# Letting GpSimd gather up to 24 tiles ahead of the sums in the middle of a graph layer, and closing up to eight at the end

## The chip, the cores and the metric

The kernel runs on one core of a Trainium2 chip. The metric is the device time of one execution in microseconds. Before the change three runs gave 1995.14, 1996.98 and 1998.15 us, so the median is 1996.98 us.

## What is computed

A layer of a relational graph network over 12500 nodes with 256 features, 212500 edges sorted by target, and 8 edge types, in float32:

```python
h   = maximum(layernorm(x), 0)
hx  = einsum('ni,rio->rno', h, weight)            # 8 types
agg = segment_sum(hx[edge_type, src], dst)        # 212500 edges
out = x + agg * 0.5**0.5 + h_bias + (h @ loop_weight) * 0.5**0.5
```

## The kernel before, in words

**Tiles and units.** The edges are cut into 1583 tiles of up to 128 edges; two tiles make a unit. The main loop runs once over the tiles, `t` from 0 to 1582. In step `t` the 128 source rows of a tile (1 KB each) lie in an SBUF tile `msg`, a one-hot matrix `oh` over (target, type) lies beside it, and TensorE multiplies them (`edge_sums`, L972) into a PSUM bank `ps`. VectorE adds the bank of a unit to a ring of accumulators `acc` (`add_sums`, L998). When a group of 128 nodes is complete, TensorE multiplies its accumulators by the 8 weight matrices and the loop weight into `po` (L1154), VectorE adds `x` (L1167, L1168), and SyncE writes every four groups out (L1173). Those products are dealt out between the sums of later tiles. All engine orders are written out by hand; no scheduler changes them.

**How the rows come.** For most tiles GpSimd issues one indirect DMA (`gather`, L885), 128 rows from `h32`, the normed table in HBM (the first 100 gathers read `x` and norm it on the core). For every 28th tile, 45 in all, GpSimd is passed by: `begin_fetch` and `load_sources` issue the 128 rows one by one, 64 from SyncE's queue and 64 from ScalarE's (L908). They are put into those queues 36 tiles ahead of their use, from eight steps later on at four per queue and step.

**What sets the lead.** At the top of step `t` the loop issues gathers until `goal(t)` is reached, and each of them is made to wait for the last unit whose sums have been written into the program (`latest["unit"]`):

```python
while gathered < min(NT, goal(t)):
    gather(gathered)
```

So a gather for tile `t + lead` does not start on the chip before the sums of about tile `t - 1` are done: `lead` is how far GpSimd may run ahead. It is 64 (`AHEAD`) up to tile 170 (`NARROW`), then shrinks by one tile in five (`SLOPE`) to `NEXT`.

**Two other waits of the same instructions.** The gathers signal their landing on eight semaphores in turn. In the built program each gather also waits until the gather eight places before it has landed, whatever `lead` is. And the message buffers are 33 pairs, handed out in turn (`room`), so the first row of a tile that is fetched row by row waits for the sums of the tiles that last used its pair. The three waits stand like this in the listing of the program before (GpSimd's gathers of tiles 612 and 613, ScalarE's first row of tile 587; semaphore values written out as tiles):

```
POOL gather of tile 612        waits: gather eight before landed; sums through tile 603
POOL gather of tile 613        waits: gather eight before landed
ACT  first row of tile 587     waits: sums through tile 503
```

Of the kernel before, what the change touches and what calls it, by code (L numbers as in the profile page):

```python
# [55 lines left out]
STEEP = 2  # L56
NARROW = 170
SLOPE = 5
NEXT = 8

SINGLE = 28
FETCH = 4
# [177 lines left out]
def kernel(  # L240
# [20 lines left out]
    NT = plan.NT  # L261
# [42 lines left out]
    with ExitStack() as main:  # L304
# [587 lines left out]
        def goal(t):  # L892

            lead = max(NEXT, AHEAD - max(0, t - NARROW) // SLOPE)
            return min(t + lead + 1, STARTED + STEEP * (t // PAIR * PAIR))

        def load_sources(t, r0, engine):
# [302 lines left out]
        with tc.manual_schedule():  # L1200
# [115 lines left out]
            for t in range(NT):  # L1316
# [3 lines left out]
                while gathered < min(NT, goal(t)):  # L1320
                    gather(gathered)
                    gathered += 1
# [122 lines left out]
```

## Time and profile before

| | us |
|---|---|
| median of three runs | 1996.98 |
| the profiled execution's own time | 1995.13 |
| its span in the profile | 1993.4 |
| TensorE matmul busy (share of the span) | 1779.7 (89%) |
| TensorE weight load busy | 1557.2 (78%) |
| GpSimd busy | 1461.3 (73%) |
| VectorE busy | 1378.2 (69%) |
| ScalarE busy | 136.1 (7%) |

A row of a group view names line, engine, operation, output and inputs and count, then busy time, mean duration in ns of one, and the idle time of the engine just before these instructions with what ended most of it. In a timeline row the figures ahead are start and duration in us, and the bracket holds the idle time just before the instruction and what ended it; "issue" means that nothing in the profile ended it. "POOL" is GpSimd, "SPq" and "ACTq" are the DMA-issuing sequencers of SyncE and ScalarE.

### The profile page before, as it was taken

Reading aid. Unit: us, or ns where it says so; the run is one execution under the profiler, and the core shown is the slowest. Engines: PE = TensorE matmul, PEld = TensorE weight load, DVE = VectorE, ACT = ScalarE, POOL = GpSimd, SP = SyncE. Lnnn points to the kernel's source line nnn. Section 1 sums busy time; section 2 is a strip of 40 time slices with the busy share of each in tenths; the row PEclk is TensorE's granted clock in tenths of the full one; section 3 lists DMA queues with packets and bytes.
Section 4 is the critical chain, followed back from the end, with each engine's and each line's share of the span. In section 5 each row is a group of like instructions: output and inputs, shape, how many; then the busy total and the mean of one; then the engine's idle time right before and its main releaser. Section 6 shows DMA issues by size and latency. Waiting matters only on the chain. (4 is left out here: it accounts for less than half of the span.)

```text
span 1993.4 us, 39889 instructions
## 1 busy us (share of the span) xinstructions
PE 1779.7 (89%) x10171; PEld 1557.2 (78%) x10171; DVE 1378.2 (69%) x3288; ACT 136.1 (7%) x243; POOL 1461.3 (73%) x1563
## 2 busy tenths in 40 slices
PE   2458999999999988999999999999999999899998
PEld 2347899899978876888878887878877887787986
DVE  6779767779856777656569666668766667765752
ACT  6764200000000000000000000000000000000000
POOL 7677777777767777777777777777777777777774
PEclk9559999999999999999999999999999999999999
DMA  8993434444444544444444444444444344444432
GB/s 269 354 289 98 143 106 138 141 136 120 139 119 118 150 130 114 136 130 123 140 119 142 131 119 139 131 129 139 132 121 142 109 141 131 117 142 118 130 106 77
DMA packets 157314, 279.57 MB, mean 140 GB/s; under 512 B 34799, under 2 KB 107864, under 8 KB 157080
## 3 DMA queue, kind: packets, MB, share of 16 engines
q0 software_dynamic: 73824, 201.69, 34.7%
q1 hardware_dynamic: 75896, 72.34, 11.7%
q10 hardware_dynamic: 7360, 2.97, 0.8%
q8 instruction: 80, 1.31, 0.3%
q14 instruction: 154, 1.26, 0.2%
HBM read 251.26 MB, written 25.60 MB: 139 GB/s over the span
## 5 line engine op out<-in xcount | busy, mean ns | idle before, releaser
L885 POOL DMA_INDIRECT msg<-h,gidx x1438 | 1364.7, 949 | 470.0 <-issue 353.8
L972 PEld LDWEIGHTS ps<-oh,msg 128*128 128x128 f32 x6332 | 995.2, 197 | 344.8 <-DMA msg<-h,gidx 206.5
L972 PE MATMUL ps<-oh,msg 128*128 128x176 f32 (+1 forms) x6332 | 1107.2, 305 | 176.2 <-DMA msg<-h,gidx 99.4
L1154 PE MATMUL po<-w,acc 128*128 128x256 f32 x3136 | 883.1, 386 | 9.4 <-DVE acc L998 9.4
L998 DVE TENSOR_TENSOR acc<-acc,ps 128x352 f32 x792 | 409.9, 518 | 369.9 <-PE ps L972 357.8
L1154 PEld LDWEIGHTS po<-w,acc 128*128 128x128 f32 x3136 | 532.1, 192 | 42.8 <-DVE acc L998 11.4
L935 DVE TENSOR_TENSOR oh<-fixed,cols 128x704 f32<-128x704 f32 x397 | 349.2, 880 | 0.0
L1036 DVE SCALAR_TENSOR_TENSOR acc<-types,pt 128x256 f32<-128x256 bf16 (+1 forms) x688 | 247.5, 413 | 85.0 <-PE pt L1018 79.8
L885 POOL DMA_INDIRECT msg<-in_x_dram,gidx x100 | 94.8, 948 | 38.8 <-issue 30.3
L1154 PE MATMUL po<-wl,self_t 128*128 128x256 f32 x392 | 111.7, 409 | 3.4 <-DVE acc L998 1.7
L1154 PEld LDWEIGHTS po<-wl,self_t 128*128 128x128 f32 x392 | 72.0, 205 | 12.9 <-DVE acc L998 2.5
L823 ACT ACTIVATE msg<-msg,shift,rstd 128x256 f32<-128x256 f32 x100 | 50.7, 586 | 4.2 <-DVE shift L820 3.4
L823 ACT ACTIVATE xt<-xt,shift,rstd 128x256 f32<-128x256 f32 x98 | 50.0, 587 | 7.0 <-DVE shift L820 5.6
L1167 DVE TENSOR_TENSOR xr<-xr,po 128x256 f32<-128x256 f32 x98 | 40.5, 414 | 13.3 <-PE po L1154 12.5
L793 DVE BATCH_NORM_STATS2 stats<-xt 128x6 f32<-128x256 f32 x98 | 34.3, 412 | 19.1 <-DMA xt<-in_x_dram 18.3
L1090 DVE CAST types<-pt 128x512 bf16<-128x512 f32 x22 | 15.2, 692 | 44.8 <-PE pt L1086 44.8
L1023 DVE COPY self_t<-pt 128x256 f32<-128x256 f32 x98 | 40.8, 416 | 6.8 <-PE pt L1018 5.5
L1018 PE MATMUL pt<-ident,hr 128*128 128x128 f32 x196 | 38.1, 277 | 7.5 <-DMA hr<-h 6.4
L1168 DVE TENSOR_TENSOR xr<-xr,po 128x256 f32<-128x256 f32 x98 | 41.2, 421 | 3.4
L429 DVE TENSOR_SCALAR moves<-fixed 128x271 int32<-128x271 int32 (+1 forms) x90 | 40.5, 451 | 3.1 <-DVE acc L998 2.1
L431 DVE COPY_PREDICATED fixed<-moves,fixed 128x311 int32<-128x311 int32 (+14 forms) x90 | 38.0, 422 | 3.1
L793 DVE BATCH_NORM_STATS2 stats<-msg 128x6 f32<-128x256 f32 x100 | 34.2, 410 | 0.0
(154 smaller groups left out, 321.1 us busy)
## 6 DMA issues: line engine op xcount, KB each, us to landing
msg<-h SPq DMA_DIRECT2D x2880, 1.0 KB
msg<-h ACTq DMA_DIRECT2D x2880, 1.0 KB
msg<-h,gidx POOLq DMA_INDIRECT x1438
xt<-in_x_dram SPq DMA_DIRECT2D x24, 512.0 KB
h<-xt SPq DMA_DIRECT2D x24, 512.0 KB
xr<-in_x_dram SPq DMA_DIRECT2D x24, 512.0 KB
hr<-h SPq DMA_DIRECT2D x24, 512.0 KB
out_dram<-xr SPq DMA_DIRECT2D x24, 512.0 KB
```

What stands on the lines that cost most here:

```text
L429: nc.vector.tensor_single_scalar(m, packed[:, :n], 1 << (bit + k), op=ALU.bitwise_and)
L793: in_run("stats", nc.vector.bn_stats(stats[:n, k, :], row), row is rows_[-1])
L823: nc.scalar.activation(row, row, AF.Relu, bias=shift[:n, j : j + 1], scale=rstd[:n, j : j + 1])
L885: i = nc.gpsimd.indirect_dma_start(out=msg[t], out_offset=None, in_=table[:, :], in_offset=bass.IndirectOffsetOnAxis(ap=gidx[b][:, at : at ...
L935: j = nc.vector.tensor_tensor(o[:, k : k + v, :i, :], iota_f.unsqueeze(1).unsqueeze(1).to_broadcast([P, v, i, C]), of.unsqueeze(3).to_broa ...
L972: j = nc.tensor.matmul(ps[:, c, :width], m[:, c * P : (c + 1) * P], o[:, :width], start=(i == 0 and c == 0), stop=(end and c == KC - 1))
L998: i = nc.vector.tensor_tensor(a, a, ps, op=ALU.add)
L1023: nc.vector.tensor_copy(got["self", g][:, :, :n], pst[:, :, :n])
L1036: i = nc.vector.scalar_tensor_tensor(acc[:, :, r, s0 : s0 + n], of, float(r + 1), pst[:, :, :n], op0=ALU.is_equal, op1=ALU.mult)
L1154: i = nc.tensor.matmul(got["out", g][:n], lhs, rhs, start=(r == R and c == 0), stop=(r == R - 1 and c == KC - 1))
L1167: nc.vector.tensor_add(rows_[:n, k, :], rows_[:n, k, :], outs[g % 2][:n, 1, :])
L1168: nc.vector.tensor_add(rows_[:n, k, :], rows_[:n, k, :], got["out", g][:n])
```

## The change

`NEXT` becomes 24, and a second line lets the lead close up towards the end of the edges to the new constant `CLOSE`, which is 8: by one tile in five over the last 120 tiles, and it stays at eight for the last forty or so.

```diff
-NEXT = 8
+NEXT = 24
+CLOSE = 8
...
         def goal(t):

             lead = max(NEXT, AHEAD - max(0, t - NARROW) // SLOPE)
+            lead = min(lead, max(CLOSE, (NT - t) // SLOPE))
             return min(t + lead + 1, STARTED + STEEP * (t // PAIR * PAIR))
```

In the built program no engine gets an instruction more or less, and on every engine the order of the instructions is the same. What differs is which semaphore values GpSimd, SyncE and ScalarE wait for. The three waits from above, after:

```
POOL gather of tile 612        waits: gather eight before landed; sums through tile 587
POOL gather of tile 613        waits: gather eight before landed
ACT  first row of tile 587     waits: sums through tile 519
```

## The prediction

> **What bounds the kernel now.** I read the page first, then the group of the message tile, then the chain that ended last.
>
> ```profile
> span 1993.4 us, 39889 instructions
> ...
> PE 1779.7 (89%) x10171; PEld 1557.2 (78%) x10171; DVE 1378.2 (69%) x3288; ACT 136.1 (7%) x243; POOL 1461.3 (73%) x1563
> ```
>
> ```profile
> L885 POOL DMA_INDIRECT msg<-h,gidx x1438: 940/946/1253, 136.4 to 1969.8; - x180
> L885 POOL DMA_INDIRECT msg<-in_x_dram,gidx x100: 940/946/1112, 4.9 to 135.2; - x100
> ```
>
> ```profile
> 1967.34 2.72 DMA msg<-h,gidx
> 1970.06 0.04 issue
> 1970.10 0.86 PE ps L972 x4
> ...
> 1979.93 7.78 PE po L1154 x36
> ...
> 1988.19 0.42 DVE xr L1168
> ```
>
> By busy time TensorE looks like the limit (89%) and GpSimd idle a quarter of the time. The other two fences correct that. GpSimd issues 1538 gathers; an undisturbed pair, below, starts 1.25 us apart (0.95 of work, 0.30 between), so they need 1537 x 1.25 = 1921 us, and from the first start (4.9) to the last (1969.8) pass 1964.9. GpSimd stands still for only some 44 us. The end hangs on its last gathers: landing, four matmuls, products that take until the last addition at 1988.2. So a microsecond that GpSimd gains in the middle and does not lose again is a microsecond at the end.
>
> TensorE can follow. These windows give TensorE's busy time first, GpSimd's fifth:
>
> ```profile
> 507.00:566.00 59.00, 57.87 (x355) 52.92 (x354) 44.04 (x97) 0.00 (x0) 40.38 (x43) 1.00 0.46 130
> 731.00:794.00 63.00, 54.27 (x294) 43.93 (x293) 50.02 (x120) 0.00 (x0) 45.54 (x48) 0.97 0.46 128
> 804.00:867.00 63.00, 58.87 (x347) 50.83 (x346) 41.10 (x91) 0.00 (x0) 47.50 (x51) 1.00 0.46 135
> 1846.00:1906.00 60.00, 59.01 (x351) 54.03 (x351) 39.29 (x88) 0.00 (x0) 44.42 (x47) 1.00 0.43 126
> ```
>
> At 804 to 867 GpSimd runs at its full rate (51 gathers in 63 us) and TensorE idles for 4 us: some 6% of room. At 507 it is 98% busy, but there it is still using up the early lead, and what GpSimd gains there it keeps as lead until TensorE has room again.
>
> **What the wait on the sums costs.** The lead was already 17 or more up to tile 400, so the change acts from about 440 us. GpSimd's waits from there to 1975 us, with the 0.30 that stands before every gather inside:
>
> ```profile
> POOL msg L885 <- issue: 298.0, 965, 2.1
> POOL msg L885 <- DMA msg<-h,gidx: 43.8, 109, 2.0
> POOL msg L885 <- PE ps L972: 37.3, 100, 1.5
> POOL msg L885 <- PE pt L1018: 5.4, 12, 1.7
> POOL msg L885 <- PE po L1154: 3.3, 9, 0.9
> ```
>
> Taking off 0.304 each (1.25 less the median 0.946): landings end 43.8 - 33.1 = 10.7 us of excess, TensorE 46.0 - 36.8 = 9.2 us over the three rows, and 298.0 - 293.4 = 4.6 us have no releaser. That is all that can be had after 440 us: 24.5 us.
>
> The 9.2 us bound the wait that the change loosens from above. From below stand the cases in which nothing else was due:
>
> ```profile
> 550.45 0.94 POOL L885 DMA_INDIRECT msg<-h,gidx  x1 [1.86 <-DMA msg<-h,gidx]
> 551.70 0.94 POOL L885 DMA_INDIRECT msg<-h,gidx  x1 [0.30 <-issue]
> ...
> 619.87 0.94 POOL L885 DMA_INDIRECT msg<-h,gidx  x1 [0.59 <-PE ps L972]
> ...
> 623.08 0.94 POOL L885 DMA_INDIRECT msg<-h,gidx  x1 [1.02 <-PE ps L972]
> ...
> 1173.78 0.94 POOL L885 DMA_INDIRECT msg<-h,gidx  x1 [1.12 <-PE ps L972]
> ...
> 1236.91 0.94 POOL L885 DMA_INDIRECT msg<-h,gidx  x1 [0.73 <-PE ps L972]
> ...
> 1871.09 0.94 POOL L885 DMA_INDIRECT msg<-h,gidx  x1 [1.67 <-PE pt L1018]
> ```
>
> Less 0.30 each, these five are 0.29 + 0.72 + 0.82 + 0.43 + 1.37 = 3.6 us. The other TensorE-ended waits lie among waits for landings, and behind them the landing of the gather eight before is due next; I count little of them and take **4 us**. The last, at 1871, is followed by no other stop. The closing of the lead costs nothing there: near tile 1502 it still stands at about 19 where eight stopped the gather, and for the last forty tiles it is what it was.
>
> **The wait for the gather eight before.** This wait stays, so a lead of 24 never means 24 gathers in flight; eight at 1.25 us is 10 us. The extra 16 tiles are used only when rows have landed and TensorE is late. Gathers that land in over 9 us stop GpSimd whatever the lead is: the 10.7 us. What makes them slow? Two stretches of the message tile, first 731 to 804 us, then 804 to 870:
>
> ```profile
> L908 ACTq DMA_DIRECT2D msg<-h x182: 227/228/787, 730.8 to 803.8; - x182
> ...
> L908 SPq DMA_DIRECT2D msg<-h x158: 227/228/480, 731.2 to 793.0; - x158
> L885 POOL DMA_INDIRECT msg<-h,gidx x54: 940/946/1131, 730.8 to 803.0; - x54
> ...
>   POOL msg L885: 10.0, 15
> ```
>
> ```profile
> L908 ACTq DMA_DIRECT2D msg<-h x140: 227/228/605, 803.8 to 869.7; - x140
> ...
> L908 SPq DMA_DIRECT2D msg<-h x128: 227/228/308, 819.7 to 869.6; - x128
> L885 POOL DMA_INDIRECT msg<-h,gidx x53: 942/946/1162, 804.2 to 869.5; - x53
> ...
>   POOL msg L885: 1.2, 4
> ```
>
> In the first, both row queues issue almost without a pause for 62 us and GpSimd waits 10.0 us for landings (with the 0.30); in the second they pause, and it waits 1.2. By the Trainium skill's "DMA: Bandwidth & Descriptors", section "Queues, rings and completion order", a DMA engine takes turns between the queues that have work, packet by packet, so a third busy queue would thin out the gathers' share; the two stretches agree. By that rule alone the landings quicken wherever one row queue pauses.
>
> **What the change does to the row queues.** No instruction moves, but the first row of a row-by-row tile now waits for sums 16 tiles later (tile 587: through 519, not 503), because the gathers take their buffers earlier. Why ScalarE's queue ran so long without a pause at 731:
>
> ```profile
> 632.72 49.77 ACTq L392 DMA_DIRECT2D spans<-in_dst_dram  x8
> 682.58 187.36 ACTq L908 DMA_DIRECT2D msg<-h  x435
> ...
> 1635.73 22.99 SPq L908 DMA_DIRECT2D msg<-h  x64
> ```
>
> It stood for 50 us at the loads of a block's spans, and then caught up with tiles whose buffers had long been free. A tile is 64 rows, 23 us of queue time (last row), in 28 tiles x 1.25 = 35 us: 12 us of pause when a queue is not behind. A gate 16 x 1.25 = 20 us later makes ScalarE's queue reach its gate one to two tiles sooner, and pause, while SyncE's, held up mostly at the output writes, goes on as before. So stretches with both queues busy for some 60 us should become stretches of 20 to 35 us, which GpSimd got through in the trace without a stop.
>
> What that is worth lies between nothing and all of 10.7 + 4.6 = 15.3 us; below nothing if the pauses fall badly (a rival). I take the middle, **8 us**: the catching up after the block at 1632 us begins so far behind that a gate 20 us later leaves its first stretch.
>
> Behind the later row issue the cover is the time to use: tile 587 is gated at the sums of 519 and used 68 tiles, 85 us, later, against 23 us of issue. SyncE's output write, its node loads and the rest of its queue stand behind these rows; they are due some 28 tiles, 35 us, before the rows' use at the earliest, so 85 - 35 = 50 us for 23 us of issue. I count nothing.
>
> **Sum.** 4 + 8 = 12 us off the profiled execution's 1995.13: 1983.1. That execution is the fast end of the three runs; the median lies 1.85 above it, so I add that: **1985 us**. Own range, from the median: 3.6 + 3 = 6.6 off gives 1990; all 24.5 off gives 1972.5.
>
> **Rivals.**
> *Only the wait on the sums goes.* The windows show that VectorE is busier where GpSimd stops: 75% and 79% at 507 and 731, 65% at 804 and 1846. The Trainium skill's "GPSIMD Engine Reference", section "Specifications", says that GpSimd shares its SBUF interfaces with VectorE; the trace cannot part that from the row queues, which are busy at the same times. If VectorE's work slows the gathers, the landings stay slow: 1996.98 - 3.6 = 1993.4 us.
> *The wait moves.* GpSimd, let go at the sums, stops a few gathers later for the landing eight back, which was due anyway; the row queues change nothing: 1997 us. For it: eight is also the depth of the landings, so the old lead of eight nearly coincides with it. Against it: 1871 and 1173, with no landing wait behind them.
> *Slower: the row queues fall into step.* ScalarE and SyncE now both start a tile's rows at one event, and both add pauses only together; landings over 9 us come in more stretches. The price: a bad stretch like 507 to 566 loses 59/1.25 - 43 = 4 gathers, 5 us. If the landing waits double, 15.3 us come on and 3.6 go: 1997 + 12 = 2009 us. It decides from about three bad stretches more than now. Against it: SyncE's queue was late on its own account throughout, so it seldom starts at the gate.
>
> **How the numbers follow.** Forecast 0.58, only the sums 0.15, wait moves 0.10, in step 0.17. A measurement of this kernel can tell about 0.2%, 4 us, from no change. 1993.4 lies at that bound: I split it, 0.07 faster and 0.08 same. Faster 0.58 + 0.07 = 0.65, same 0.08 + 0.10 = 0.18, slower 0.17. The range reaches over the first rivals to 2000 and leaves out the last and the forecast's lowest end: 1975 to 2000. The forecast alone would be 1972.5 to 1990.
>
> **What would show it.** Right: GpSimd's waits ended by TensorE after 440 us shrink from 9.2 us of excess to under 2; landing waits shrink to about half; the gaps before gathers at 1871 and 1173 read 0.30; ScalarE's row queue shows pauses around 750 to 830 us; the last gather starts near 1958. Wrong: landing waits as long or longer, in new stretches where both row queues are busy; matmuls that wait for rows of L908; or TensorE busy all through while GpSimd is 20 tiles ahead, so that GpSimd no longer sets the end.

## The result, and the profile after

| | before | after |
|---|---|---|
| median of seven runs, us | 1996.98 | 1984.88 |
| lowest and highest, us | 1990.56, 2000.73 | 1982.09, 1989.28 |
| profiled execution, us | 1995.13 | 1985.18 |
| its span, us | 1993.4 | 1983.5 |

The ratio is 0.994, with a 95% interval of 0.9923 to 0.9957: 12 us off the median, against a forecast of 1985. In two of the four sets of runs below the kernel before took about 2397 us, so every ratio is against the kernel before of its own set, and those two sets are told apart from the others.

The page after, and the group of the message tile (lines lie one or two further down than before):

```profile
span 1983.5 us, 39925 instructions
...
PE 1765.5 (89%) x10171; PEld 1548.6 (78%) x10171; DVE 1377.0 (69%) x3288; ACT 136.0 (7%) x243; POOL 1463.2 (74%) x1563
```

```profile
L886 POOL DMA_INDIRECT msg<-h,gidx x1438: 940/946/1252, 136.3 to 1959.7; - x180
L886 POOL DMA_INDIRECT msg<-in_x_dram,gidx x100: 940/946/1109, 4.9 to 135.1; - x100
```

GpSimd did the same work in the same time, and its last gather starts at 1959.7 instead of 1969.8: it comes 10.1 us earlier, and the span is 9.9 us shorter. What follows that gather is as long as before. The page counts 36 instructions more (39925 against 39889). All of them are separate semaphore waits, 18 each in the streams of SyncE and ScalarE; the count of every other kind of instruction is the same, so "no instruction more or less" above holds only without these waits. GpSimd's waits from 440 to 1975 us:

```profile
POOL msg L886 <- issue: 293.0, 951, 2.1
POOL msg L886 <- DMA msg<-h,gidx: 43.6, 119, 1.3
POOL msg L886 <- PE ps L974: 29.8, 95, 0.9
POOL msg L886 <- PE po L1156: 6.4, 19, 0.9
POOL msg L886 <- PE pt L1020: 3.4, 11, 0.3
```

Less 0.304 for each gather, as in the prediction, landings leave 43.6 - 36.2 = 7.4 us, TensorE (with three rows of 0.9 and less) 41.7 - 40.1 = 1.6, no releaser 293.0 - 289.1 = 3.9: 12.9 us in all, where it was 24.5. The waits that the view puts under TensorE shrank as forecast; those for landings fell by a third, from 10.7 us, and not to half. The gathers that stopped at 1173.78 and 1871.09 before are these two; both now start without a stop:

```profile
1163.86 0.95 POOL L886 DMA_INDIRECT msg<-h,gidx  x1 [0.30 <-issue]
...
1860.97 0.95 POOL L886 DMA_INDIRECT msg<-h,gidx  x1 [0.30 <-issue]
```

The lead of 24 was never used up here. Counting at each gather from tile 460 to 1462 how many tiles it is ahead of the last finished sums gives a median of five and at most ten in the profile after (six and nine before).

### The profile page after: what moved, and what is told of

It is laid out like the page before. It is cut to its first block, busy times and chain, and to the rows that moved or that the text cites. A ratio compares the mean times of both kernels' runs of the same rounds, so it can differ in the third digit from the quotient of the medians.

```text
span 1983.5 us, 39925 instructions
## 1 busy us (share of the span) xinstructions
PE 1765.5 (89%) x10171; PEld 1548.6 (78%) x10171; DVE 1377.0 (69%) x3288; ACT 136.0 (7%) x243; POOL 1463.2 (74%) x1563
## 3 DMA queue, kind: packets, MB, share of 16 engines
q10 hardware_dynamic: 7360, 2.97, 0.8%
```

## The experiments

**The lead alone.** The kernel before, its gathers in their old places of the program, so that buffers and row gates stay; only the sums that a gather waits for lie further back:

```diff
             if "unit" in latest:
+                far = min(24, max(8, (NT - t) // SLOPE))
+                unit = units.get((t - far - 1) // PAIR) if t >= 400 else None
                 tc.add_manual_dep(
-                    i.ins, latest["unit"], SYNC_DEP, reason="no faster than the sums")
+                    i.ins, unit or latest["unit"], SYNC_DEP, reason="no faster than the sums")
...
```

> The kernel before, in which a gather of tile 400 or later waits for sums 24 tiles back instead of eight (closing up at the end as in the change), while the gathers stay where they stood in the program, so that buffers and the row queues' gates are those of before (tile 587: sums through 503). Theory (the wait on the sums and the later row gates each bring a part): the waits that TensorE ended go, landing waits stay, 3.6 to 7 us faster, ratio 0.997. Rival, the lead brings it all: 12 us, ratio 0.994. Rival, the row gates bring it all: 1.000.

Measured: 0.9984 (0.997 to 0.9999); the profiled span is 1988.3 us.

**The row gates alone.** The kernel before, lead eight; the first row that each row queue issues for a tile waits for the sums 68 tiles ahead of it (`GATE` is 68):

```diff
...
+                if i == 0 and t >= 419:
+                    tc.add_manual_dep(
+                        j.ins, units[(t - GATE) // PAIR], SYNC_DEP, reason="rows start later")
...
```

> The kernel before with its lead of eight, in which the first row that each queue issues for a row-by-row tile waits for the sums 68 tiles ahead of it instead of 84, as in the changed kernel. Theory: TensorE-ended waits stay, landing waits shrink by about 5 us, ratio 0.997. Rival, the lead brings it all: 1.000, landing waits as before. Rival, the gates bring it all: ratio 0.994.

Measured: 0.9974 (0.9962 to 0.9986); span 1986.5 us. The product of the two ratios is 0.9958, the change 0.994 (0.9923 to 0.9957) in its own set. So each brings a part, and the two add up within what the intervals allow. That one of them brings it all lies outside both intervals; that the lead brings nothing lies outside by 0.0001 only, and for that the waits below are the better evidence.

GpSimd's waits show a trap. First the lead alone, then the row gates alone:

```profile
POOL msg L885 <- issue: 286.1, 928, 3.0
POOL msg L885 <- DMA msg<-h,gidx: 44.8, 129, 1.5
POOL msg L885 <- PE ps L974: 44.5, 114, 2.0
```

```profile
POOL msg L886 <- issue: 294.0, 956, 1.7
POOL msg L886 <- DMA msg<-h,gidx: 38.6, 108, 2.7
POOL msg L886 <- PE ps L976: 38.4, 103, 1.9
```

The lead alone still seems to wait 44.5 - 34.7 = 9.8 us for sums, although the sums that its gathers wait for had long been done. One such row of its timeline:

```profile
574.24 0.95 POOL L885 DMA_INDIRECT msg<-h,gidx  x1 [0.30 <-issue]
577.19 0.94 POOL L885 DMA_INDIRECT msg<-h,gidx  x1 [2.01 <-PE ps L974]
578.44 0.94 POOL L885 DMA_INDIRECT msg<-h,gidx  x1 [0.30 <-DMA msg<-h,gidx]
```

This is tile 445. By the semaphore events the gather eight before it landed 0.76 us earlier; the sums that it waits for were done 22.9 us earlier. The view names the engine whose semaphore moved last before the start, and TensorE's moves all the time. So I read every delayed gather against both events. A gather that waited starts 0.27 us after the sums, or 0.26 or 0.76 us after the landing. Summed over the gathers from tile 340 on, in us beyond the ordinary gap, with the number of gathers, beside the total of the waits view (which also holds 1 to 1.5 us of gaps that are a few ns too long):

| kernel | landing eight back | sums | neither | total by the view | span |
|---|---|---|---|---|---|
| before | 14.5 (28) | 6.7 (11) | 2.0 | 24.5 | 1993.4 |
| lead alone | 16.1 (30) | 0 | 2.8 | 20.2 | 1988.3 |
| row gates alone | 9.3 (18) | 4.4 (4) | 1.4 | 16.3 | 1986.5 |
| the change | 9.8 (18) | 0 | 1.8 | 12.9 | 1983.5 |
| ScalarE's single rows left out | 0 | 3.2 (5) | 0 | 4.1 | 1971.0 |
| the change, spans by SyncE | 2.7 (6) | 0 | 2.1 | 6.0 | 1973.6 |

Against the kernel before, each kernel's span and total standstill fall by the same amount within 2 us: GpSimd's standstill accounts for the differences of the span. These are single profiles, and the one of the kernel before is from the set in which it took 1996.98 us; in the set of the experiments it took 1992.47. The lead takes all waits on sums, and the waits for landings come out 1.6 us longer; the gates take 5.2 us of waits for landings and 2.3 us of those on sums.

**Row queue or VectorE.** What slows the landings? In the kernel before, ScalarE's 64 rows of a tile become two loads of 32 consecutive rows, so the indexed half of these tiles is left out:

```diff
+            if engine is ACT:
...
+                    j = nc.scalar.dma_start(
+                        msg[t][r0 : r0 + SOURCES, :].bitcast(U8),
+                        h32[r0 : r0 + SOURCES, :].bitcast(U8))
...
+                fetches[engine].insert(0, (0, fetch_block))
+                return
...
-                j = nc.tensor.wait_ge(counters[k % COUNTERS], 16 * P * (k // COUNTERS + 1))
+                j = nc.tensor.wait_ge(counters[k % COUNTERS], 16 * (P // 2 + 2) * (k // COUNTERS + 1))
```

> The kernel before, in which ScalarE's 64 single rows of each of the 45 row-by-row tiles are replaced by two loads of 32 consecutive rows (the wrong rows: the indexed half of these tiles is left out), so that the two row queues are never busy together. Theory (two busy row queues slow the gathers' landing): GpSimd's landing waits after 440 us fall from some 11 us of excess to under 2, and the kernel is 8 to 12 us faster, ratio 0.995, the sums' waits staying or growing. Rival (VectorE's work slows the gathers): landing waits as before, ratio 1.000.

Measured: 0.9919 (0.9898 to 0.9939). GpSimd's waits, then the windows of all engines, VectorE's busy time third:

```profile
POOL msg L885 <- issue: 295.6, 970, 0.3
POOL msg L885 <- PE ps L988: 52.3, 161, 2.1
POOL msg L885 <- DMA msg<-h,gidx: 8.5, 28, 0.3
```

```profile
731.00:794.00 63.00, 59.51 (x350) 51.62 (x349) 53.81 (x145) 0.00 (x0) 47.76 (x51) 1.00 0.41 118
804.00:867.00 63.00, 59.09 (x350) 51.61 (x349) 41.13 (x92) 0.00 (x0) 47.75 (x51) 1.00 0.41 118
```

The landing waits are 8.5 us in 28, the ordinary 0.30. In 731 to 794 VectorE is busier than before (53.8 of 63 us against 50.0) and GpSimd keeps its full rate of 51 gathers (48 before). So VectorE's work alone does not make the landings late; the second busy row queue is needed. It isn't the bytes: by its page ScalarE's queue (q10) moves 2.96 MB, before 2.97 MB, about 1% of all bytes, in 5920 packets instead of 7360. How single rows from a second queue slow the landings, no run here shows.

Nor are two busy row queues enough. VectorE's busy time (third) and GpSimd's (fifth) in the kernel before, in three stretches with both row queues busy:

```profile
455.00:502.00 47.00, 47.00 (x295) 44.23 (x294) 44.12 (x124) 0.00 (x0) 35.61 (x38) 1.00 0.44 121
508.00:566.00 58.00, 56.87 (x350) 52.00 (x349) 43.07 (x96) 0.00 (x0) 39.69 (x42) 1.00 0.46 128
974.00:1036.00 62.00, 56.45 (x313) 47.04 (x313) 36.48 (x77) 0.00 (x0) 46.88 (x50) 0.97 0.45 127
```

GpSimd lost some 6 us in the second and nothing in the other two, one of them longer, the other with VectorE 94% busy. What else decides stays open.

**Spans by SyncE.** In the changed kernel, SyncE issues the small loads behind which ScalarE's rows stood:

```diff
-            queue = nc.scalar if b > 1 else nc.sync
+            queue = nc.sync
```

> The changed kernel, in which SyncE issues the small loads of a block's spans that stood in ScalarE's queue, so that ScalarE's rows need not wait behind them and catch up afterwards. Theory: the two stretches with both row queues busy for some 60 us (727 to 790 and 1672 to 1728 in the profile after) break up, and GpSimd's stops in them, some 6 us, mostly go: 0.991 of the kernel before, against 0.994 for the change. Rival (those stretches come from something else, or SyncE falls behind by the moved loads): 0.994 or more.

Measured: 0.992 (0.9904 to 0.9936). Again, in a later set:

> The changed kernel with the spans' loads by SyncE, again, for a chip on which the kernel before takes some 2400 us. Theory: GpSimd's rate does not set the end there, TensorE's late rows and instructions do, so the gain is gone: 1.000, between 0.998 and 1.003. Rival (the gain carries over): 0.992, as where the kernel before takes some 1992 us.

The kernel before took 1996.42 us in that set, not 2400, so its theory wasn't put to the test; the ratio was 0.9907 (0.9893 to 0.9922), at 1978.52 us. This version is faster than the kernel before in both sets. It was not run beside the change, whose 0.994 (0.9923 to 0.9957) overlaps the first interval. The message tile from 727 to 790 us shows how, first the change, then with the spans by SyncE:

```profile
L910 SPq DMA_DIRECT2D msg<-h x158: 227/228/683, 727.4 to 789.2; - x158
L910 ACTq DMA_DIRECT2D msg<-h x152: 227/228/836, 726.9 to 788.6; - x152
...
L886 POOL DMA_INDIRECT msg<-h,gidx x48: 942/946/1105, 727.1 to 788.8; - x48
...
  POOL msg L886: 9.3, 16
```

```profile
L910 SPq DMA_DIRECT2D msg<-h x158: 227/228/304, 728.4 to 790.0; - x158
...
L910 ACTq DMA_DIRECT2D msg<-h x102: 213/214/453, 736.3 to 789.7; - x102
L886 POOL DMA_INDIRECT msg<-h,gidx x51: 942/946/1162, 726.2 to 789.2; - x51
...
  POOL msg L886: 2.4, 8
```

SyncE issues the same 158 rows; ScalarE, no longer behind, 102 instead of 152; GpSimd gets 51 gathers through instead of 48.

**The closing, the spans without the change, and more tiles row by row.** `no_closing` is the change without its second line, `before_spans_by_sync` the kernel before with SyncE issuing the spans, `spans_single24` the change with the spans by SyncE and `SINGLE = 24`.

> The changed kernel without its second line: the lead stays at 24 to the end of the edges. Theory: no gather waits for the sums in the last 120 tiles at 24 or while closing up, so the ratio is that of the change, 0.994. Rival (a lead of 24 at the end costs something that the closing saves): slower than the change by 2 us or more, 0.995 or above.

> The kernel before, lead of eight and old buffers, with the spans' loads issued by SyncE instead of ScalarE. Theory: the row gates are early as before, but ScalarE no longer falls behind, so the long stretches around 731 and 1676 to 1811 us break up; landing waits shrink by some 6 us, TensorE-ended waits stay: ratio 0.996. Rival (the gain of the spans' loads needs the later gates): 0.999 or more.

> The changed kernel with the spans by SyncE and every 24th tile fetched row by row instead of every 28th (53 tiles instead of 45). GpSimd issues 8 gathers fewer, 10 us at 1.25 each; a tile's rows take 23 us of 30 instead of 35 us on either queue. Theory (GpSimd's rate sets the end): 0.987 to 0.990 of the kernel before. Rival (the row queues, with less pause, slow the landings again or come too late): 0.992 or more, with landing waits or matmuls waiting for rows.

In this set the kernel before took 2398.52 us; the ratios were 1.007 (1.0044 to 1.0097), 1.0024 (1.0004 to 1.0044) and 1.0622 (1.0584 to 1.066), none as its theory has it. All three were run once more, with the change itself beside them:

> The changed kernel without its second line again, beside the change itself (in the run before, the kernel before took 2398 us, and each instruction queue issued more slowly). Theory: as the change, 0.994 of the kernel before, no gather waiting for the sums at the end. Rival: 0.996 or more.

> The changed kernel itself, as measure for the other three. Theory: 0.994 of the kernel before where that takes some 1997 us; where it takes some 2400 us, with row-by-row tiles arriving late, 1.00 or more, since the later row gates then cost.

> The kernel before with the spans' loads issued by SyncE, again. Theory: landing waits shrink by some 6 us, TensorE-ended waits stay, ratio 0.996. Rival (the gain of the spans' loads needs the later gates): 0.999 or more.

> Every 24th tile row by row, lead 24, spans by SyncE, again. Theory: 8 gathers fewer, 0.987 to 0.990. Rival (rows come too late): 0.992 or more, TensorE waiting at L970 or L972 for rows.

The kernel before took 2395.77 us here: 1.0078 (1.0049 to 1.0108) without the closing, 1.0005 (0.9987 to 1.0023) for the change, 1.0022 (0.9998 to 1.0046) for the kernel before with the spans by SyncE, 1.0615 (1.0589 to 1.0641) with 53 tiles row by row. It isn't the chip: the set at 2398.52 us and the one at 1996.42 ran on the same one. What is different in these sets, in the changed kernel: the chain that ended last, by engine; TensorE's waits; a stretch of SyncE's queue; last, TensorE's waits with 53 tiles.

```profile
SPq 34%; issue 26%; PE 26%; DVE 7%; another core or an unknown queue 3%; DMA 2%; ACT 1%; POOL 0%; DVEq 0%; PEldq 0%; ACTq 0%; POOLq 0%
```

```profile
PE ps L974 <- issue: 164.2, 230, 3.3
PE po L1156 <- issue: 88.3, 122, 5.4
PE ps L974 <- PEq L971: 56.5, 14, 9.6
```

```profile
1231.82 51.95 SPq L910 DMA_DIRECT2D msg<-h  x84
1283.80 0.68 SPq L1175 DMA_DIRECT2D out_dram<-xr  x1
...
1324.76 45.87 SPq L910 DMA_DIRECT2D msg<-h  x86
```

```profile
PE ps L974 <- PEq L971: 326.7, 39, 13.8
PE ps L974 <- issue: 119.7, 145, 4.7
```

A row takes SyncE 0.53 to 0.62 us (45.87 / 86, 51.95 / 84) instead of 22.99 / 64 = 0.36. At that rate a tile's 64 rows take 34 to 40 us, and the 28 tiles from one such tile to the next take GpSimd 35. SyncE's last row of such a tile has been issued 2.2 us (median) before the tile's last multiplication, where it is 18.7 us in the profile after. The rows come late, TensorE stands at L971, which waits for them, and stands much longer with more such tiles. GpSimd is then 21 tiles (median) ahead of the sums: it does not set the end, and the change is worth nothing. So in this condition `no_closing`, 1.0078 against 1.0005 for the change, says that the closing is worth some 0.7%. In the two profiles of this set both kernels finish the sums of tile 1463 at 2230 us, and those of the last tile at 2382 with the closing and 2397 without it; the granted clock over the last stretch of some 560 multiplications was 1.00 and 0.96. Its mechanism is open. Where the kernel before takes 1997 us, the closing alone and the spans alone remain unmeasured, and so do 53 tiles; in the profile after, GpSimd is at most nine tiles ahead in the last 120 tiles, so the closing had little to hold back there.

## Why the prediction was right

- **What bounds the kernel** was right: in every kernel that freed GpSimd the last gather moved by as much as the end, and the span shrank by GpSimd's standstill within 2 us. It held only in the sets where SyncE's queue issues a row in some 0.36 us, which the trace of before could not show.
- **The sum** hit 1984.88 almost to the point, and that is luck: its two terms were off in opposite directions. The waits on sums, sized at 4 us, were 6.7 us gather by gather, and the change took them all. The waits for landings, sized at 8 us, fell by 4.7 us (14.5 to 9.8). By the waits view it is 9.2 - 1.6 = 7.6 us and 15.3 - 11.3 = 4.0.
- **The wait on the sums** alone, by `lead_only`: 0.16% (0.01 to 0.3%), 3.2 us of 1992.47, since some of it came back as waits for landings. The five quoted cases were clean. Those among the landing waits, of which the prediction counted little, were another 3 us; the rest of the bound of 9.2 was mainly landings under TensorE's name.
- **The row gates** alone, by `gate_only`: 0.26% (0.14 to 0.38%), 5.2 us, or 7.3 us by the medians of that set. The mechanism was right: landings come sooner. But 2.3 us of what they took were waits on sums, which the prediction had put under the lead. Whether both together bring more than the two alone isn't shown: the intervals allow it, and by the standstills they don't (24.5 - 20.2 = 4.3 and 24.5 - 16.3 = 8.2 us alone, 11.6 together).
- **Which stretches break up** was wrong. ScalarE's queue did pause between 750 and 830 us, from 774 to 778 and from 802 to 811, but the stretch from 727 stayed (152 rows, 9.3 us of landing waits in the fence above, 10.0 before). After its stand at the spans the queue was 29.5 us behind even the later gate (tile 587), and it caught up only with tile 671. The landing waits that went were at 509 to 580 us (5.5 to 3.5 us), around 1345 (0.9 to nothing) and around 1805 (1.6 to nothing).
- **Stretches of 20 to 35 us cost nothing**, the premise of that term, did not hold in general: in the profile after, both queues are busy from 511 to 535 and from 540 to 564 us, and GpSimd loses 4.1 us there.
- **The last gather** was foreseen near 1958 and started at 1959.7.
- **Rivals.** "The wait moves" was right for 1.6 us of the 6.7. VectorE as the only cause of late landings fell with ScalarE's rows. The row queues did not fall into step: from tile 363 on, SyncE's first row of a tile started 25 us or more behind its gate in the profile after.
- **Not foreseen**: a condition in which the change is neutral (1.0005), and in which the closing, counted at nothing, is what keeps it neutral.

## What to carry to other kernels

An engine that is 73% busy by the page can still set the end: count its instructions times their spacing, not their busy time, and what is left is all that any change to its waits can bring, as long as that engine keeps setting the end. A change of a lead also moves when buffers are taken, and with them every other transfer that waits for those buffers; list the waits of the built program before and after on all queues, and cost each that moved. When a view names a releaser, test it against the time of the event that the instruction really waits for.

## What the hardware showed beside this

- With both row queues busy (the median over the gathers begun then, from 340 to 1875 us) a gather landed 5.2 us after its issue ended, with one busy 3.0, with none 1.8, in the kernel before; of the stretches of 55 us and more with both busy, two cost GpSimd some 6 and 5 us (from 508 and 731 us), the others 2 us or less, and the one from 974 to 1036 us nothing.
- In the sets at some 2397 us the same median in the changed kernel was 1.6 us, with none, one or both queues busy: rows were issued more slowly and the gathers landed sooner. What slowed the issue there stays open.
